# Layer 0's loads written later in the program, four layers' weights loaded one by one, fewer and larger late blocks

## The chip, the cores and the metric

The kernel runs on one core of a Trainium2 chip as a single launch. The metric is the device time in microseconds (us); lower is better.

## The reference

A graph network of four layers over N = 2708 nodes with D = 128 features and one adjacency matrix `adj` of 2708 x 2708 float32, of which under 1% is not zero. Each layer normalises the rows of x, applies relu, and adds its result to x:

```python
h = relu(layernorm(x)); x = x + L0(h, adj)   # (adj.T @ h) / column sums of adj
h = relu(layernorm(x)); x = x + L1(h, adj)   # sum over j of adj[i,j] * gelu(s[i] + d[j] + msg_b), then upd_w, gelu, layernorm
h = relu(layernorm(x)); x = x + L2(h, adj)   # adj @ h, W_msg, relu, then a GRU cell (W_ih, W_hh and biases)
h = relu(layernorm(x)); x = x + L3(h, adj)   # two attention heads over adj > 0 (ff0, attn, ff1, g1, b1, g2, b2)
```

## The kernel before

Rows go in 22 tiles of 128 (the last has 20), in six groups of four tiles (`GROUPS`; the last group has two). The order of work on each engine is the order in which the program is written.

**Layer 0** (up to about 223 us) reads the whole of `adj` once, as 30 sets (c, s), a window of columns c (0 to 4) by a group of rows s (0 to 5), in the order of the list `order`; set 6c + s is its number here. The last 228 columns (window 5, `LAST`) are loaded apart, into `z0` to `z5`, and worked on between the sets of window 4. For each set:

- SP's queue loads `a` (`load_cut`, L318, or L324 for the short group) into a ring of `RING = 5` buffers, so that a load waits for the set five before it.
- DVE finds the eight largest values of each row in every block of 124 columns and their places (`list_cut`, L358 and L360); GpSimd (POOL) masks the blocks near the diagonal first (`mask_near`).
- PE transposes the set (`p_T`, L396) in up to four turns and adds `a` times h to the window's sums (L382). A turn goes into one of three PSUM banks (`turnp`).
- ACT evacuates a turn to `aT` (L401) with the column sums as a by-product, and then issues the write of the turn before it to `adjT` in HBM from its own queue (`write_one`, L366). Layers 2 and 3 read `adjT`.
- When a window is done, DVE inverts its column sums (`inv_deg`, L431), and the window's part of x is formed. After the last window, PE transposes the sums (`p_s`, L449), which waits for a DVE block that ends with `ends` (L637).

Between the sets, ACT also works on rows of x (L254, L264, L136). Every transfer that SP's or ACT's queue issues takes one of eight completion semaphores, in rotation in the order of the program over both queues, and waits until the transfer eight before it, which has the same semaphore, is done. An ACT instruction behind such a write waits with it.

Layer 1's weights are loaded at set 3 (`(c, s) == (0, 3)`, L590 to L593), those of layers 2 and 3 at set 15 (`(2, 3)`, `load` L90 and `load_columns` L97), all from SP's queue.

**Layer 1** (about 255 to 590 us) goes over the 22 row tiles in `period(t)`, each with steps k. For each tile it lists the non-zero entries, gathers the columns' features with matmuls on PE, applies gelu on ACT and adds up again with matmuls. ACT copies the column numbers (`where_T`, L844), which SP passes through HBM (`passed` L846, `spread`). The blocks of 124 columns that layer 0 had no time to list, the late blocks, are loaded from `adj` by `load_late` at k = 4, one period ahead: `AT_ONCE = 5` blocks for a period, each in a transfer of its own (`cols_a`), and listed on DVE by `list_late`. Layers 2 and 3 follow from about 600 us on.

Of the kernel before, what the change touches and what calls it, by code (L numbers as in the profile page):

```python
# [51 lines left out]
def size(t):  # L52
    return min(P, N - t * P)


def width(b):
    return min(JB, N - b * JB)
# [3 lines left out]
def listed_layers(ctx: ExitStack, tc: tile.TileContext, x, adj, w, out, flag):  # L61
# [23 lines left out]
    ident = const.tile([P, P], F32, name="ident")  # L85
    make_identity(nc, ident)

    def load(pool, name, shape=None):
        t = pool.tile(list(shape or w[name].shape), F32, name=name)
        nc.sync.dma_start(t, w[name])  # L90
        return t

    def load_columns(pool, name):

        k = w[name].shape[0] // P
        t = pool.tile([P, k], F32, name=name)
        nc.sync.dma_start(t, w[name].rearrange("(k p) -> p k", p=P), allow_slow_non_contiguous=True)  # L97
        return t

    def load_rows(pool, name):  # L100

        t = pool.tile([P, w[name].shape[0]], F32, name=name)
        nc.sync.dma_start(t, w[name].partition_broadcast(P))
        return t


    minus_half = const.tile([P, NT], F32, name="minus_half")
# [175 lines left out]
            yield  # L283

    RING = 5
    WINDOW = CH + 16 * (len(GROUPS) - 2)
    l0, ending = ExitStack(), ExitStack()
    ordered = ExitStack()
# [253 lines left out]
    for i, (c, s) in enumerate(order):  # L542
        g0, gk = GROUPS[s]
        if i == len(order) - 1:
            for n in range(4):
                list_last(n)
            count_some(0, FIRST)
            count_some(FIRST, 1)
        list_cut(c, s, g0)
        if i == 0:  # L550
            state["f", 0] = factors(*state.pop(("m", -1)))
            list_cut(c, s, g0 + 1)
            state["m", 1] = moments(tiles_of(xs, *GROUPS[1]), "n4")
            list_cut(c, s, g0 + 2)
            state["f", 1] = factors(*state.pop(("m", 1)))
            list_cut(c, s, g0 + 3)
        else:
            for n in range(g0 + 1, g0 + gk):
                if c > 0 and s == (1 if c < LAST - 1 else 0) and n == g0 + 2:
                    invert(c - 1)  # L560
                list_cut(c, s, n)
        if i + 1 < len(order):
            mask_near(*order[i + 1])
        if i > 0 and i - 1 + RING < len(order):
            load_cut(*order[i - 1 + RING])
        if c == LAST - 2:
            load_cut(LAST, s)
        if c > 0 and s == (2 if c < LAST - 1 else 1):
            turn_sums(c - 1)
        if (c, s) == (LAST - 1, LAST):  # L570
            turn_rows(LAST - 2)
            ranked = rank(0, FIRST, bank("p_r"))
            turn_sums(LAST)
        work_cut(c, s, first_steps(s) if c == 0 else next_steps(c, s))
        if c > 1 and s == 0:
            turn_rows(c - 2)
        if c > 1 and s == 1:
            destinations(c - 2)
        if c > 1 and s == 3:
            split_destinations(c - 2)  # L580
        if c == LAST - 1:
            for z in PARTS.get(s, ()):
                mask_near(LAST, z)
                work_cut(LAST, z)
            if s == LAST - 1:
                for _ in lift(LAST):
                    pass

        if (c, s) == (0, 3):
            nc.sync.dma_start(msg_wT, w["msg_wT"])  # L590
            nc.sync.dma_start(upd_wT, w["upd_wT"])
            for v, name in ((upd_b, "upd_b"), (ln_w, "ln_w"), (ln_b, "ln_b"), (msg_b, "msg_b")):
                nc.sync.dma_start(v, w[name].partition_broadcast(P))  # L593
        if (c, s) == (2, 3):
            W_msgT, W_ihT, W_hhT = load(late, "W_msgT"), load(late, "W_ihT"), load(late, "W_hhT")
            b_msg, b_ih, b_hh = load_columns(late, "b_msg"), load_columns(late, "b_ih"), load_columns(late, "b_hh")
            ff0T, ff0, ff1T = load(late, "ff0T"), load(late, "ff0"), load(late, "ff1T")
            attn = load_columns(late, "attn")
            gain1, shift1, gain2, shift2 = (load_columns(late, v) for v in ("g1", "b1", "g2", "b2"))
            nc.gpsimd.tensor_copy(src_self[:, 0, :], msg_wT[:, 0, :])  # L600
            nc.gpsimd.tensor_tensor(src_self[:, 1, :], msg_wT[:, 0, :], msg_wT[:, 1, :], ALU.add)

# [47 lines left out]
    destinations(LAST - 2)  # L650
    l0.close()

    gate_b = late.tile([P, 2], F32, name="gate_b")
    half_b = late.tile([P, 1], F32, name="half_b")

# [20 lines left out]
    with (  # L676
# [25 lines left out]
        def load_late(t):  # L702

            units = late_blocks[(t - 1) * AT_ONCE : t * AT_ONCE] if t > 0 else []
            if not units:
                return
            cols = work.tile([P, AT_ONCE, JB], F32, name="cols_a")
            state["late", t] = []
            for i, (n, b) in enumerate(units):
                m, k = size(n), width(b)  # L710
                nc.sync.dma_start(cols[0:m, i, 0:k], adj[n * P : n * P + m, b * JB : b * JB + k])
                state["late", t].append((n, b, cols[0:m, i, 0:k]))

        def list_late(t, first, last):
            units = state.get(("late", t), [])[first:last]
# [312 lines left out]
        def period(t, between=()):  # L1028

            now, c, b, a = (0 <= t + q < NT for q in range(4))  # L1030
            last = 0 <= t - 1 < NT
            if c and not between:
                put_values(t + 1)
            for k in range(GB):
                for step in between[k : k + 1]:
                    step()
                if now:
                    combine(t, k)
                if k == (0 if t else 1) and c:
                    pass_on(t + 1)  # L1040
                if k == 1 and a:
                    nc.vector.tensor_copy(*rank(t + 3, 1, rpool.tile([P, CH], F32, tag="r", name="p_r")))
                    spread_ends(t + 3)
                if k == 1 and last:
                    gather(t - 1, GB - 2)
                elif k in (3, 5) and now:
                    gather(t, k - 3)
                if now:
                    activate(t, k)
                if k == 1 and last:  # L1050
                    gather(t - 1, GB - 1)
                    close_tile(t - 1)
                elif k in (3, 5) and now:
                    gather(t, k - 2)
                if k == 1:
                    if now and t % 2 == 0 and t + 2 < NT:
                        project(t // 2 + 1)
                if (t, k) in mixes:
                    mix(mixes[t, k])
                if k in (1, 2) and b:  # L1060
                    fetch(t + 2, k - 1)
                if k == 1 and a:
                    lead_of(*values_of(t + 3))
                if k == 1:
                    list_late(t, 0, EARLY)
                    if t == WIDE_AT:
                        list_wide()
                if k == 2:
                    if now and t % 2 == 0 and t + 2 < NT:
                        sources(t // 2 + 1)  # L1070
                    if a:
                        select_rows(t + 3)
                        describe_rest(t + 3)
                    if now and t % 2 == 0 and t + 2 < NT:
                        sources_rest(t // 2 + 1)
                    if now and t + 4 < NT - 2:
                        count_rows(t + 4)
                if k == 1 and t == NT - 2:
                    check_lists()
                if k > 0 and c:  # L1080
                    put_more(t + 1, k)
                if k == 3 and c:
                    columns(t + 1)
                if k == 3 and t == WIDE_AT:
                    place_wide()
                if k == 3 and b:
                    place(t + 2)
                if k == 4 and a:
                    finish_rows(t + 3)
                if k == 4:  # L1090
                    load_late(t + 1)
                    if t + 1 == WIDE_AT:
                        load_wide()
                for g, step in updates.pop((t, k), ()):
                    update(g, step)
                if k == GB - 1:
                    list_late(t, EARLY, AT_ONCE)
                    if now and NT - 2 <= t + 4 < NT:
                        count_rows(t + 4)
# [28 lines left out]
        if True:  # L1128
            period(0)
            for t in range(1, NT + 1):  # L1130
                period(t)
            assert not updates
        puts.close()
    lists.close()

# [874 lines left out]
```

## Time and profile before

| | us |
|---|---|
| median of three runs | 1023.68 (1022.53 to 1025.39) |
| the profiled execution | 1026.56 |
| its span | 1024.8 |
| busy: PE, DVE, ACT, POOL | 925.0, 796.3, 533.6, 460.2 |

The profile is of one execution, on one core. A span of 1024.8 in 40 slices makes one slice 25.6 us. Names like `a` stand for all buffers of that name. The engine SP issues transfers only; its rows are marked SPq, and ACT's issues ACTq. A wait names what ended it, inferred from the semaphores. `adj`'s loads of layer 0 are 1.0 to 1.15 MB for a full set, an `adjT` write 256 KB, a late block 62 KB.

### The profile page before, as it was taken

The page shows a single profiled execution, that of the slowest core. Times are in us where ns is not written, and L with a number is a line of the kernel's source. Part 1 is how long each engine was busy: PE and PEld are TensorE (multiplying, and loading weights), DVE is VectorE, ACT ScalarE, POOL GpSimd, SP SyncE. Part 2 cuts the span into 40 slices and gives each one's busy share as a digit, 9 for nine tenths or more (in the row PEclk, how much of TensorE's full clock was granted, in tenths as well). Part 3 has the DMA queues.
Part 4 walks back from the last instruction along what each step waited for, and adds up shares of the span by engine and source line. Part 5 has one row for each costly group of instructions (what it writes and reads, how often), then busy time and mean ns, then how long its engine had stood idle before and what let it go on. Part 6 is the DMA issues. An engine that isn't in the chain of part 4 may idle for free. (4 is left out here: it accounts for less than half of the span.)

```text
span 1024.8 us, 22209 instructions
## 1 busy us (share of the span) xinstructions
PE 925.0 (90%) x7948; PEld 748.9 (73%) x7948; DVE 796.3 (78%) x2753; ACT 533.6 (52%) x1561; POOL 460.2 (45%) x588
## 2 busy tenths in 40 slices
PE   6699898964899999999899999999889999999983
PEld 3354454733799999999899844444578999989972
DVE  7998784976788898998976566666578977997793
ACT  5655546744667566767666523323322543664342
POOL 6322122322887777897976364433211300340042
PEclk9998989965899999999999999999899999999996
DMA  9899899613244334443332366555311475457000
GB/s 334 266 309 318 263 350 379 224 68 113 75 135 139 123 116 120 131 137 102 109 114 105 108 217 217 176 198 195 85 45 56 144 222 187 139 169 234 7 15 16
DMA packets 88954, 165.42 MB, mean 161 GB/s; under 512 B 20432, under 2 KB 35908, under 8 KB 88834
## 3 DMA queue, kind: packets, MB, share of 16 engines
q1 hardware_dynamic: 68854, 131.77, 40.2%
q10 hardware_dynamic: 19980, 32.14, 8.6%
q8 instruction: 64, 1.05, 0.4%
q14 instruction: 56, 0.46, 0.1%
HBM read 117.26 MB, written 30.87 MB: 145 GB/s over the span
## 5 line engine op out<-in xcount | busy, mean ns | idle before, releaser
L1219 PE MATMUL att<-hv,wt 128*128 128x129 f32 x1672 | 195.5, 278 | 7.4 <-DVE wt L1189 5.9
L825 POOL TENSOR_SCALAR put<-count,line,value 128x128 f32<-128x128 f32 x176 | 195.1, 1120 | 11.7 <-PE agg L938 10.6
L1219 PEld LDWEIGHTS att<-hv,wt 128*128 128x128 f32 x1672 | 191.8, 194 | 10.5 <-DVE wt L1189 8.5
L913 PE MATMUL p_m<-s,sel 128*128 128x128 bf16 x1452 | 162.6, 220 | 6.5 <-ACT g L925 4.0
L917 PE MATMUL p_m<-d,cols 124*128 124x128 bf16 (+1 forms) x1452 | 162.9, 221 | 3.8 <-DVE cols L856 3.8
L1189 DVE SCALAR_TENSOR_TENSOR wt<-row,lift,mask 128x1024 f32<-128x1024 f32 (+1 forms) x132 | 138.8, 1082 | 23.0 <-PE att L1219 22.9
L120 POOL TENSOR_TENSOR n_r<-n_r,minus_half 128x4 f32<-128x4 f32 (+1 forms) x28 | 39.5, 1412 | 243.4 <-DVE n_r L119 238.2
L382 PE MATMUL sums<-a,h 128*128 128x512 f32 x220 | 124.4, 664 | 1.6 <-ACT h L136 1.6
L938 PE MATMUL agg<-put,g 128*128 128x128 f32 (+1 forms) x968 | 122.5, 279 | 0.0
L396 PEld LDWEIGHTS p_T<-ident,a 128*128 128x128 f32 (+1 forms) x440 | 57.3, 149 | 83.2 <-issue 42.7
L938 PEld LDWEIGHTS agg<-put,g 128*128 128x128 f32 x968 | 113.2, 192 | 0.0
L1380 PE MATMUL p_agg<-a,hs 128*128 128x512 f32 (+2 forms) x264 | 107.9, 550 | 3.4 <-DMA a<-adjT 3.4
L913 PEld LDWEIGHTS <-sel 128*128 128x128 bf16 x1452 | 104.1, 98 | 7.9 <-issue 7.2
L917 PEld LDWEIGHTS <-cols 124*128 124x128 bf16 (+1 forms) x1452 | 103.2, 98 | 4.9 <-DVE cols L856 4.9
L925 ACT ACTIVATE g<-p_m 128x512 f32<-128x512 f32 x132 | 72.7, 553 | 59.5 <-PE agg L938 42.8
L834 ACT ACTIVATE put<-mine,value 128x128 f32<-128x128 bf16 x308 | 100.7, 393 | 0.0
L396 PE MATMUL p_T<-ident,a 128*128 128x128 f32 (+1 forms) x440 | 75.2, 292 | 26.7 <-ACT aT L401 20.2
L401 ACT ACTIVATE aT<-p_T 128x512 f32<-128x512 f32 (+2 forms) x132 | 71.0, 539 | 37.4 <-PE p_T L396 27.9
L1380 PEld LDWEIGHTS p_agg<-a,hs 128*128 128x128 f32 (+1 forms) x264 | 47.4, 193 | 50.4 <-issue 45.4
L360 DVE FIND_INDEX8 col<-val,a 128x8 uint16<-128x124 f32 x306 | 82.3, 281 | 0.0
L1342 ACT ACTIVATE hs<-hs 128x1354 f32<-128x1354 f32 (+1 forms) x44 | 58.5, 1329 | 41.6 <-DMA hs<-in_adj 41.2
L358 DVE MAX8 val<-a 128x8 f32<-128x124 f32 x306 | 70.8, 272 | 2.4 <-DMA a<-in_adj 2.4
(291 smaller groups left out, 1568.7 us busy)
## 6 DMA issues: line engine op xcount, KB each, us to landing
hs<-in_adj SPq DMA_DIRECT2D x42, 677.0 KB
adjT<-aT ACTq DMA_DIRECT2D x105, 256.0 KB
a<-adjT SPq DMA_DIRECT2D x20, 1280.0 KB
spread<-passed SPq DMA_DIRECT2D x22, 704.0 KB
later<-sel SPq DMA_DIRECT2D x22, 616.0 KB
a<-in_adj SPq DMA_DIRECT2D x5, 1152.0 KB
a<-in_adj SPq DMA_DIRECT2D x5, 1120.0 KB
a<-in_adj SPq DMA_DIRECT2D x5, 1088.0 KB
```

The source lines that it names most:

```text
L360: nc.vector.max_index(col[0:m, n, b, :], val[0:m, n, b, :], v)
L382: nc.tensor.matmul(accs[c][:, 0:w], h0[0:m, n, :], a[0:m, n - g0, t0 * P - lo : t0 * P - lo + w], start=(n == 0), stop=(n == NT - 1),)
L396: nc.tensor.transpose(p[0:k, i * iw + q * P : i * iw + q * P + m], a[0:m, q, e : e + k], ident[0:m, 0:m])
L825: nc.gpsimd.tensor_scalar(st["put", 0][:, b, :], count, st["line"][:, b : b + 1], st["value"][:, b : b + 1], ALU.is_equal, ALU.mult,)
L834: nc.scalar.activation(st["put", 1][:, b - HP, :], st["mine"][:, b - HP, :], AF.Identity, scale=st["value"][:, b : b + 1])
L913: nc.tensor.matmul(p[:, b - b0, :], st["sel"][:, b, :], s3[:, q, t % 2, :], start=(q == 0), stop=False)
L917: nc.tensor.matmul(p[:, b - b0, :], st["cols"][0:kb, b, :], d3[0:kb, b, q, :], start=False, stop=(q == 2))
L925: nc.scalar.activation(g[:, 0:n, :], state[t].pop(("p", k))[:, 0:n, :], AF.Gelu)
L938: nc.tensor.matmul(agg, g[:, b - 4 * k, :], put, start=(b == 0), stop=False)
L1189: nc.vector.scalar_tensor_tensor(wt[:, 0:n], row[:, k, c : c + n], lift[:, j, k : k + 1], mask[:, j, c : c + n], op0=ALU.max, op1=ALU.mult,)
L1219: nc.tensor.matmul(banks[s // 3][:, s % 3, :], wt[:, q * P : (q + 1) * P], hv[:, j, k, :], start=(v < 2 and s // 3 not in touched), stop=( ...
L1380: nc.tensor.matmul(pa[:, 0:n], h[0:k, j, :], a[0:k, j - j0, 0:n], start=(j == 0), stop=(j == NT - 1))
```

## The change

It has three parts.

- *Layer 0's loads.* In the written program, the load of set j stands at set j − 2 and no longer at set j − 4 (`BEHIND = 2`). The ring still has five buffers. The loads of `z0` to `z5` stay at the sets of window 3, and so come before `a` loads that they came after.
- *Weights.* Of the six transfers at set 3 only `msg_wT` is left, at set 8, and `msg_b`, at set 15. The other 18 (`upd_wT`, `upd_b`, `ln_w`, `ln_b` of layer 1 and all of layers 2 and 3) are put on the list `waiting`; `load_next` issues one of them at k = 0 and one at k = 3 of each period of layer 1 until the list is empty.
- *Late blocks.* Neighbouring blocks of the same tile are loaded in one transfer, and always for 128 rows.

```diff
+    waiting = []
+
+    def load(pool, name):
+        t = pool.tile(list(w[name].shape), F32, name=name)
+        waiting.append((t, w[name], {}))
         return t
...
+    def load_next():
+        if waiting:
+            t, v, how = waiting.pop(0)
+            nc.sync.dma_start(t, v, **how)
...
     RING = 5
+    BEHIND = 2
...
-        if i > 0 and i - 1 + RING < len(order):
-            load_cut(*order[i - 1 + RING])
+        if i > BEHIND and i - 1 - BEHIND + RING < len(order):
+            load_cut(*order[i - 1 - BEHIND + RING])
         if c == LAST - 2:
             load_cut(LAST, s)
...
-        if (c, s) == (0, 3):
+        if (c, s) == (1, 2):
             nc.sync.dma_start(msg_wT, w["msg_wT"])
-            nc.sync.dma_start(upd_wT, w["upd_wT"])
-            for v, name in ((upd_b, "upd_b"), (ln_w, "ln_w"), (ln_b, "ln_b"), (msg_b, "msg_b")):
-                nc.sync.dma_start(v, w[name].partition_broadcast(P))
         if (c, s) == (2, 3):
-            W_msgT, W_ihT, W_hhT = load(late, "W_msgT"), load(late, "W_ihT"), load(late, "W_hhT")
...
+            nc.sync.dma_start(msg_b, w["msg_b"].partition_broadcast(P))
...
+    waiting.append((upd_wT, w["upd_wT"], {}))
+    for v, name in ((upd_b, "upd_b"), (ln_w, "ln_w"), (ln_b, "ln_b")):
+        waiting.append((v, w[name].partition_broadcast(P), {}))
+    W_msgT, W_ihT, W_hhT = load(late, "W_msgT"), load(late, "W_ihT"), load(late, "W_hhT")
...
-                m, k = size(n), width(b)
-                nc.sync.dma_start(cols[0:m, i, 0:k], adj[n * P : n * P + m, b * JB : b * JB + k])
-                state["late", t].append((n, b, cols[0:m, i, 0:k]))
+                state["late", t].append((n, b, cols[0 : size(n), i, 0 : width(b)]))
+            i = 0
+            while i < len(units):
+                n, b = units[i]
+                k = 1
+                while i + k < len(units) and units[i + k] == (n, b + k) and width(b + k) == JB:
+                    k += 1
+                if width(b) < JB:
+                    nc.sync.dma_start(cols[:, i, 0 : width(b)], adj[n * P : (n + 1) * P, b * JB : b * JB + width(b)])
+                else:
+                    nc.sync.dma_start(
+                        cols[:, i : i + k, :],
+                        adj[n * P : (n + 1) * P, b * JB : (b + k) * JB].rearrange("p (b e) -> p b e", e=JB),
+                    )
+                i += k
...
+                if k in (0, 3):
+                    load_next()
                 if k == 4:
                     load_late(t + 1)
```

More of the change, by code (lines that the diff above doesn't have):

```diff
@@ L86, in listed_layers @@
     make_identity(nc, ident)
-    def load(pool, name, shape=None):
-        t = pool.tile(list(shape or w[name].shape), F32, name=name)
-        nc.sync.dma_start(t, w[name])
+    waiting = []
+    def load(pool, name):
+        t = pool.tile(list(w[name].shape), F32, name=name)
+        waiting.append((t, w[name], {}))
         return t
@@ L96, in load_columns @@
         t = pool.tile([P, k], F32, name=name)
-        nc.sync.dma_start(t, w[name].rearrange("(k p) -> p k", p=P), allow_slow_non_contiguous=True)
+        waiting.append((t, w[name].rearrange("(k p) -> p k", p=P), dict(allow_slow_non_contiguous=True)))
         return t
[L100 to L104, printed above, removed]
+    def load_next():
+        if waiting:
+            t, v, how = waiting.pop(0)
+            nc.sync.dma_start(t, v, **how)
     minus_half = const.tile([P, NT], F32, name="minus_half")
@@ L587, in listed_layers @@
                     pass
-        if (c, s) == (0, 3):
+        if (c, s) == (1, 2):
             nc.sync.dma_start(msg_wT, w["msg_wT"])
-            nc.sync.dma_start(upd_wT, w["upd_wT"])
-            for v, name in ((upd_b, "upd_b"), (ln_w, "ln_w"), (ln_b, "ln_b"), (msg_b, "msg_b")):
-                nc.sync.dma_start(v, w[name].partition_broadcast(P))
         if (c, s) == (2, 3):
-            W_msgT, W_ihT, W_hhT = load(late, "W_msgT"), load(late, "W_ihT"), load(late, "W_hhT")
[L596 to L599, printed above, removed]
+            nc.sync.dma_start(msg_b, w["msg_b"].partition_broadcast(P))
             nc.gpsimd.tensor_copy(src_self[:, 0, :], msg_wT[:, 0, :])
@@ L651, in listed_layers @@
     l0.close()
+    waiting.append((upd_wT, w["upd_wT"], {}))
+    for v, name in ((upd_b, "upd_b"), (ln_w, "ln_w"), (ln_b, "ln_b")):
+        waiting.append((v, w[name].partition_broadcast(P), {}))
+    W_msgT, W_ihT, W_hhT = load(late, "W_msgT"), load(late, "W_ihT"), load(late, "W_hhT")
+    b_msg, b_ih, b_hh = load_columns(late, "b_msg"), load_columns(late, "b_ih"), load_columns(late, "b_hh")
+    ff0T, ff0, ff1T = load(late, "ff0T"), load(late, "ff0"), load(late, "ff1T")
+    attn = load_columns(late, "attn")
+    gain1, shift1, gain2, shift2 = (load_columns(late, v) for v in ("g1", "b1", "g2", "b2"))
     gate_b = late.tile([P, 2], F32, name="gate_b")
@@ L1131, in listed_layers @@
                 period(t)
-            assert not updates
+            assert not updates and not waiting
         puts.close()
```

## The prediction

> **What bounds the kernel now.** I read the page's slices first, since the change touches layers 0 and 1 only.
>
> ```profile
> PE   6699898964899999999899999999889999999983
> PEclk9998989965899999999999999999899999999996
> DMA  9899899613244334443332366555311475457000
> ```
>
> A slice is 25.6 us. Layer 0 is the first nine slices, and the only stage where the DMA row stands at 8 or 9 while PE falls under 9 and the clock under full. Layer 1 (slices 10 to 23) has PE at 9 and DMA at 2 to 4. Windows price both; the columns are the stretch, busy PE, PEld, DVE, ACT, POOL, then clock, DMA share and GB/s:
>
> ```profile
> 75.00:80.00 5.00, 5.00 (x25) 2.89 (x24) 5.00 (x34) 2.82 (x12) 0.22 (x1) 1.00 1.04 400
> 126.37:136.50 10.13, 10.10 (x20) 4.62 (x21) 4.55 (x30) 5.46 (x22) 2.80 (x9) 0.50 0.99 323
> 170.87:215.30 44.43, 39.28 (x227) 27.11 (x225) 44.18 (x289) 31.51 (x109) 13.78 (x40) 1.00 0.64 237
> 260.00:560.00 300.00, 290.35 (x4192) 286.04 (x4192) 252.77 (x690) 201.58 (x619) 246.33 (x254) 0.99 0.37 116
> ```
>
> Layer 1 is PE's (290 of 300 us). In layer 0 no engine is full throughout: for 10 us PE works at half its clock, and the last 44.4 us before layer 0's end are DVE's (44.18 busy). What starts that block is in the waits of 0 to 250 us (engine, tile, line, releaser; total, count, longest):
>
> ```profile
> DVE inv_deg L431 <- ACT aT L401: 26.1, 3, 14.5
> PE p_T L396 <- ACT aT L401: 20.6, 17, 2.8
> ACT junk L264 <- DMA a<-in_adj: 7.9, 2, 4.0
> PE p_s L449 <- DVE ends L637: 3.5, 1, 3.5
> ACT junk L264 <- DMA W_hhT<-in_W_hhT: 3.2, 1, 3.2
> ```
>
> PE waits for ACT's evacuations, DVE for ACT's column sums (its longest wait ends at 170.87, after which it runs to 215.29 and releases PE's p_s at 215.43). ACT in turn waits for transfers that its instruction doesn't read: the timeline puts its adjT write just ahead of each stall.
>
> ```profile
> 38.93 0.33 ACTq L366 DMA_DIRECT2D adjT<-aT  x1
> 39.30 0.40 ACT L264 ACTIVATE junk<-xs,flat 128x128 f32<-128x128 f32 x1 [3.92 <-DMA a<-in_adj]
> ...
> 123.59 0.40 ACT L264 ACTIVATE junk<-xs,flat 128x128 f32<-128x128 f32 x1 [3.25 <-DMA W_hhT<-in_W_hhT]
> ...
> 124.71 0.92 PE L396 MATMUL p_T<-ident,a 128*128 128x128 f32 x4 [2.80 <-ACT aT L401]
> 126.40 1.32 PE L396 MATMUL p_T<-ident,a 128*128 128x128 f32 x4 [0.78 <-ACT aT L401]
> ```
>
> In the built program every DMA of both queues takes one of eight semaphores in turn and waits for the one eight before it. So an ACT write stalls ACT until a load or weight on SP's queue lands; ACT's evacuations stand behind it, three PSUM banks later PE stands too, and the clock drops after that. Such ACT stalls sum to some 25 us in layer 0 (3.92 at 35.4, 4.02 at 79.0, 1.62 + 3.25 + 0.63 at 117 to 125, 4.14 at 142.3, 2.46 at 150, 3.20 at 170.8, two under 1).
>
> **What the Trainium skill says.** "TensorE: Matmul & The Clock Gate", "What's actually happening": the clock is halved by default and after an idle window of about 3.4 us, and comes back after a busy one. The trace agrees on the value (0.50) but not on the length: the gap before 126.37 was 2.80 us with 0.78 close behind, and the half clock lasted 10.1 us. "DMA: Bandwidth & Descriptors", "Issuing engines are not separate DMA queues": transfers of all issuers share the same 16 engines. The trace agrees: loads on SP's queue and writes on ACT's together stop at 400 GB/s with the share at 1.04. The same page, "Rules for kernel authors": coalesce many small transfers. Layer 1's late blocks are 62 KB each, but nothing is seen waiting for them.
>
> **The change, part by part.**
>
> *Loads of layer 0 (BEHIND).* In the built programs PE, ACT, DVE and POOL have the same instructions in the same order. The `a` loads keep their order on SP's queue, and each still waits for the set five before it; the SP timeline has most of them 0.03 us behind that buffer's last product already. Loads land 12 to 23 us before PE's first transpose of them. So the two sets by themselves: 0. What moves is `z`: each of the six last-column loads now stands two `a` loads earlier in SP's queue.
>
> *Weights out of layer 0.* Six small transfers at 33.66 to 36.83 become one msg_wT later, and 14 at 114.07 to 126.25 become msg_b alone:
>
> ```profile
> 113.64 0.37 SPq L318 DMA_DIRECT2D a<-in_adj  x1
> 114.07 0.51 SPq L90 DMA_DIRECT2D W_msgT<-in_W_msgT  x1
> ...
> 116.10 0.49 SPq L97 DMA_DIRECT2D b_msg<-in_b_msg  x1
> 120.93 0.38 SPq L97 DMA_DIRECT2D b_ih<-in_b_ih  x1
> ...
> 126.37 5.76 SPq L318 DMA_DIRECT2D a<-in_adj  x3
> ```
>
> - First block (A). With six transfers fewer in the rotation, the write that waited for set 7's load (35.38 to 39.30) becomes one four writes later, by when that load has landed. In its wake set 4 took PE 11.61 us (40.81 to 52.42) against 7.33 for sets 2 and 3, so 4.28, plus the 1.28 ahead of it: 5.6. Early stalls are partly taken up later, so I count 5 (0 to 6).
> - Second block (B). The ACT stalls for adjT, W_hhT and ff0T go, with PE's gaps 2.80 + 0.78 = 3.58, and the half clock 126.37 to 136.50, which costs half its length, 5.1: 8.7; I count 8 (3 to 9). Loads 20 and 21 are no longer held 10.2 and 5.8 us behind free buffers (116.20 to 126.37, 121.91 to 127.69); they were in time anyway, and only relax the queue.
> - `z` earlier (C). The `a` loads 22, 24, 25, now interleaved with the `z` loads, have the ACT write that waits for them only 3 to 5 writes (about 3.5 to 6 us) behind their issue, where loads took 7 to 11 us from issue to landing. ACT stalls like 142.31 to 146.46 and 170.83 to 174.03 come back in other places. The trace of before can't show this: between 0 and 10 us lost, of which I take 3.
> - Bytes. About 1.1 MB leave a stage that runs near its DMA peak: 1.1/400 = 2.8 us, part of A and B, not added.
>
> *Where layer 0's gain can be lost.* The stages from the end of set 23 on are fixed: DVE's block of 44.4 us stays, so what counts is how much earlier ACT ends set 23 (170.84). DVE has room: its three waits at inv_deg sum to 26.1 us, so up to 26 us pass through before DVE's own lists are the limit. After the block the order is as before, PE's clock is low across the change of layers (6 and 5 in slices 9 and 10) in both.
>
> *Weights in layer 1.* 18 transfers, one at k = 0 and one at k = 3 of the first nine periods, on SP's queue. In front of them SP mostly waits for ACT, as its waits in 255 to 600 us show, and DMA is at 0.37.
>
> ```profile
> SPq L846 <- ACT where_T L844: 100.3, 20, 15.1
> ```
>
> At 0.4 to 0.9 us an issue (rows above) 18 cost SP about 9 us over nine periods of some 15 us. Cover: SP's wait for where_T. The first used (upd_wT) is needed periods after it was issued, layer 2's at about 600. 0 (0 to 3 lost, if a weight holds up SP's index transfers behind it).
>
> *Late blocks.* 80 transfers become 21: 59 issues fewer on SP at some 0.5 us, so 30 us off a queue that waits 100 us, and 2480-byte rows for 496-byte ones. Nothing waits for them: 0 (0 to 2 gained).
>
> **Sum.** 5 + 8 − 3 = 10 gained. The profiled execution is 1026.56 (span 1024.8 and 1.76 around it): 1016.6. That execution is 2.88 above the median, 1023.68, so **1013.7** against the runs.
>
> **Rivals.**
>
> 1. *Nothing to speak of.* The rotation stays, so ACT's stalls find other loads; layer 0 as a whole moves its bytes at about 310 GB/s against 400. For: the stall 79.0 to 83.0 (load 13, issued 72.26) stands in the built order as before, and nothing touches it. Then only the bytes count: 1023.68 − 3 = about 1021. On the edge of what can be told. That the change doesn't do what it says is half true: the loads' two sets do nothing in the built order.
> 2. *Slower.* With z loads interleaved between loads 22 to 26, five ACT stalls of about 4 us each replace two. PE tolerates 2.4, so five gaps of 1.6 = 8, and each second one brings a half-clock window of about 10 us, which costs 5: 13 more, 21 lost in sets 16 to 23 against 13 won: 1023.68 + 8 = about 1031. This decides where loads take over about 6.3 us from issue while their write is four behind; against it, without the weights these loads find less on the engines, and DVE's 14.46 us of room takes nothing, because set 23 itself would be late.
> 3. *More.* Relieved from set 7 on, the loads run earlier and the stall at 79.0 to 83.0 with the half clock at 85.3 to 95.5 goes too: PE's gap there 1.54 + 10.2/2 = 6.6, and C costs nothing: 5 + 8 + 6.6 = 20: about 1004.
>
> **How the numbers follow.** My forecast has 0.50, rival 3 has 0.20, rival 1 has 0.17, rival 2 has 0.13. 0.3% of 1023.68 is 3.1 us, about what a measurement of this kernel can tell from no change. Forecast and rival 3 lie below 1020.6, and a third of rival 1: faster 0.74. The rest of rival 1, and a part of 2: same 0.14. Slower 0.12. The range goes from rival 3 (1003) to just past no change (1025), leaving out most of rival 2 and what is beyond 20 gained.
>
> **What would show it.** Right: no ACT wait on a weight; full clock at 47.7 to 51.1 and 126 to 136; DVE's waits at inv_deg down from 26.1 to about 16 with its last one ending near 160; then again a block of 44 us, PE's p_s at about 205, layers 1 to 3 as long as before. Wrong: new ACT waits on DMA z or a between 125 and 165 (rival 2), or a layer 1 that grows, with SP or DVE waiting for cols_a or a weight.

## The result, and the profile after

The changed kernel takes 1017.24 us (1016.58 to 1017.67) against 1023.74 us: a ratio of 0.9935, with a 95% interval of 0.9918 to 0.9952. That is 6.5 us faster; the forecast was 1013.7, 10 us faster, in a range of 1003 to 1025. A second measurement beside its parts (e7 below) gave 0.9941 (0.9920 to 0.9961).

The profiled execution took 1016.94 us with a span of 1015.1, 9.6 us under the one shown of before. Single executions of the kernel before, 35 of them beside e1 to e4, ran from 1019.36 to 1030.73, so a difference of two traces is not yet the difference of two kernels; the second trace of before (e11) will matter for that.

The page's slices after (25.4 us each):

```profile
PE   6799898945899999999899999999889999999983
PEclk9998999955999999999999999999899999999996
DMA  9899998413444443434223266655301574457000
```

DMA stands at 8 or 9 up to the seventh slice, as before, and is down to 4 in the eighth, where it was at 6: layer 0's traffic ends earlier. The clock of the sixth slice (127 to 152 us) is up from 8 to 9. Some of the waits of 0 to 250 us follow (engine, tile, line, releaser; total, count, longest). Line numbers here are those of the changed kernel: in layer 0 most are one or two larger, and L637 is now L632.

```profile
DVE inv_deg L433 <- ACT aT L403: 22.1, 3, 12.8
PE p_T L398 <- ACT aT L403: 19.6, 14, 3.1
ACT hT L152 <- DMA a<-in_adj: 4.8, 1, 4.8
ACT hs L137 <- DMA z<-in_adj: 4.7, 1, 4.7
PE p_s L451 <- DVE ends L632: 4.5, 1, 4.5
ACT part_x L462 <- DMA a<-in_adj: 4.1, 1, 4.1
ACT junk L265 <- DMA a<-in_adj: 3.8, 1, 3.8
```

No weight is among the releasers any more. But ACT's waits on transfers haven't shrunk: summed over 20 to 185 us they are 27.0 us before and 28.8 after. They stand behind other transfers now.

The stretches that the prediction named, in the windows (busy PE, PEld, DVE, ACT, POOL, clock, DMA share, GB/s):

```profile
47.70:51.10 3.40, 3.40 (x12) 1.57 (x13) 3.40 (x25) 1.38 (x11) 3.00 (x11) 1.00 0.96 200
126.37:136.50 10.13, 9.77 (x41) 5.44 (x40) 10.13 (x70) 5.34 (x17) 3.91 (x14) 0.83 1.08 389
162.80:207.03 44.23, 37.72 (x219) 26.11 (x217) 43.98 (x289) 30.78 (x109) 13.58 (x40) 0.98 0.59 223
260.00:560.00 300.00, 293.52 (x4247) 289.56 (x4244) 250.63 (x688) 202.20 (x619) 243.44 (x252) 1.00 0.38 122
```

The half clock is gone from the first stretch and mostly from the second, where it covers 3.4 of the 10.1 us and PE now does 41 instructions in place of 20. DVE's last block starts 8.1 us earlier (162.80 for 170.87) and has the same length (44.23 for 44.42). Its end releases PE's p_s at 207.17, 8.3 us earlier than 215.43.

PE's instructions are the same in both kernels, so the end of the n-th matmul of a tile can be set against its counterpart. PE's lead over the first trace of before, in us:

| at (us of before) | 30 | 55 | 75 | 100 | 132 | 150 | 190 | 250 | 560 | 720 | 750 |
|---|---|---|---|---|---|---|---|---|---|---|---|
| lead | 0.0 | 5.7 | 4.5 | 5.4 | 12.5 | 8.9 | 9.3 | 8.2 | 8.2 | 7.7 | 9.6 |

The lead comes in two steps, at the places of the two weight blocks (the second reaches 13.6 at 135), and each step is partly given back within 20 us. Layer 1 adds and takes nothing in this pair of traces: 8.2 at both its ends.

### The profile page after: what moved, and what is told of

Read it like the earlier page. It is cut to its first block, busy times and chain, and to the rows that moved or that the text cites. A ratio compares the mean times of both kernels' runs of the same rounds, so it can differ in the third digit from the quotient of the medians.

```text
span 1015.1 us, 22140 instructions
## 1 busy us (share of the span) xinstructions
PE 915.4 (90%) x7948; PEld 743.6 (73%) x7948; DVE 795.6 (78%) x2753; ACT 531.3 (52%) x1561; POOL 458.8 (45%) x588
## 5 line engine op out<-in xcount | busy, mean ns | idle before, releaser
L840 POOL TENSOR_SCALAR put<-count,line,value 128x128 f32<-128x128 f32 x176 | 198.8, 1141 | 11.6 <-PE agg L953 10.5
L384 PE MATMUL sums<-a,h 128*128 128x512 f32 x220 | 118.9, 637 | 1.6 <-ACT h L137 1.6
L398 PE MATMUL p_T<-ident,a 128*128 128x128 f32 (+1 forms) x440 | 72.4, 286 | 25.6 <-ACT aT L403 19.2
```

The source lines that it names most:

```text
L384: nc.tensor.matmul(accs[c][:, 0:w], h0[0:m, n, :], a[0:m, n - g0, t0 * P - lo : t0 * P - lo + w], start=(n == 0), stop=(n == NT - 1),)
L398: nc.tensor.transpose(p[0:k, i * iw + q * P : i * iw + q * P + m], a[0:m, q, e : e + k], ident[0:m, 0:m])
L840: nc.gpsimd.tensor_scalar(st["put", 0][:, b, :], count, st["line"][:, b : b + 1], st["value"][:, b : b + 1], ALU.is_equal, ALU.mult,)
```

## The experiments

Theory: the gain is that ACT no longer stands behind weight transfers in layer 0; the z loads' earlier place costs some of it; late blocks and the weights in layer 1 are free. Rivals: the z loads' order, or layer 1, carries a good part. A third rival has no run: that the weights' bytes, 1.1 MB less in a stage with a DMA share of 0.92, count by themselves, whoever stalls (the prediction put them at 2.8 us, as a part of A and B). The measured ratios, each to runs of the kernel before on the same chip:

| | kernel | us | ratio (95%) |
|---|---|---|---|
| e1 | before + weights moved | 1015.37 | 0.9919 (0.9894 to 0.9944) |
| e2 | before + loads two sets later | 1026.57 | 1.0027 (1.0004 to 1.0050) |
| e3 | before + late blocks merged | 1022.55 | 0.9984 (0.9965 to 1.0002) |
| e4 | changed, loads as before | 1015.34 | 0.9910 (0.9887 to 0.9934) |
| e5 | before + first weight block moved | 1022.18 | 0.9979 (0.9965 to 0.9993) |
| e6 | before + second block moved | 1019.30 | 0.9952 (0.9936 to 0.9967) |
| e7 | changed, again | 1018.32 | 0.9941 (0.9920 to 0.9961) |
| e8 | e4 + adjT writes on SP's queue | 1015.00 | 0.9915 (0.9884 to 0.9947) |
| e9 | e4 + z two loads later | 1014.29 | 0.9889 (0.9860 to 0.9918) |
| e10 | e8 + seven aT buffers | 1009.11 | 0.9835 (0.9810 to 0.9860) |
| e12 | e10 + z two loads later | 1005.92 | 0.9815 (0.9791 to 0.9838) |

### The parts one by one (e1 to e4)

e1 has the change's hunks for the weights alone; e3 has the one in `load_late` alone. e2 and e4 differ from before and from the changed kernel in one number each:

```diff
 # e2, in the kernel before
-        if i > 0 and i - 1 + RING < len(order):
-            load_cut(*order[i - 1 + RING])
+        if i > 2 and i - 3 + RING < len(order):
+            load_cut(*order[i - 3 + RING])
 # e4, in the changed kernel
-    BEHIND = 2
+    BEHIND = 0
```

> The kernel before with the weights moved alone (both blocks; loads of a and z written as before, late blocks in single transfers). My theory, that the whole gain comes from ACT no longer standing behind weight transfers in layer 0: about 6 to 8 us under the kernel before, so 1016 to 1018, with PE's lead over before 5.7 us at set 5 and 9 to 10 us at set 23, as in the changed kernel. Rival, that z and the late blocks carry half of it: about 1020.

> The kernel before with the loads of layer 0 written two sets later alone; in the built program only the six z loads move, each two a loads earlier. My theory: no gain, since the weights still stand ahead of load 20 and the ACT stalls at 35 and 117 to 125 stay: 1022 to 1027. Rival, that freeing the order of the z loads is where the gain comes from: 1018 to 1020.

> The kernel before with the late blocks of a tile in one transfer alone (21 for 80). My theory: nothing waits for them and SP's queue has 100 us to spare in layer 1, so within 1 us of the kernel before. Rival, that SP's queue or DVE's wait for cols_a matters in layer 1: 2 to 3 us faster, with layer 1 shorter by that.

> The changed kernel with the loads of layer 0 written as before (BEHIND = 0): weights moved and late blocks merged. If the z loads' earlier place costs the 3 us that the prediction set for it: about 1014. If it costs nothing: 1017, as the changed kernel. If it is needed for the gain: 1020.

The weights alone bring 9.0 us between medians, more than the whole change. The loads written two sets later cost 2.2 between medians when made alone, and taking them out of the change (e4) gains as much as the weights alone. Late blocks: the interval holds no change, so they may be worth up to 3.6 us or nothing; that e4, which has them, is no faster than e1 makes nothing the likelier. So of the three parts one carries the gain and one takes some of it back.

That the two sets move the z loads alone, as the prediction and e2's expectation have it, is not so. Whatever SP's queue issues between the `a` loads now stands two of them earlier. In e2 the block of six starts at 21 us in place of 34, and the block of 14 at 92 in place of 114; in the changed kernel `msg_wT` goes out at 53.49, in e4 at 63.61. So e2, and the step from e4 to the changed kernel, price z together with these.

What the gain consists of can be read from PE. It does the same work in the same order in all these kernels, so its time from one matmul to another is its idle time plus its busy time, and its busy time for the same work differs with the clock. The windows go from the product that ends at 29.8 us to the last of the eight transposes that start at 166.37 in the first trace of before (set 23). They are of before, e11 (before again), e1, the changed kernel and e7 (changed again), in this order:

```profile
29.79:167.96 138.17, 122.57 (x494) 67.70 (x492) 110.50 (x733) 81.22 (x306) 37.73 (x109) 0.90 0.92 309
29.80:162.17 132.37, 117.03 (x493) 65.42 (x492) 110.25 (x734) 79.58 (x301) 36.94 (x107) 0.94 0.94 318
29.84:157.78 127.94, 115.06 (x493) 64.53 (x492) 110.08 (x733) 80.11 (x305) 37.11 (x108) 0.95 0.92 324
29.80:158.32 128.52, 114.24 (x493) 64.25 (x492) 109.96 (x733) 78.98 (x301) 36.93 (x107) 0.96 0.94 323
29.70:155.45 125.75, 111.53 (x493) 63.05 (x492) 109.84 (x733) 78.91 (x301) 37.08 (x107) 0.99 0.96 333
```

Length less busy time is the idle time. With layer 0 as before it is 15.6, 15.3 and, in e3, 15.7 us; with the weights out 12.9 (e1) and 12.4 (e4); in the changed kernel 14.3 and 14.2. So the weights take some 3 us out of PE's waits, and the loads' part puts 1.3 to 1.9 back. The rest is the clock: take off the share of the length that it withheld (0.10 of 138.17 in the first line), and 109 to 110 us of busy time remain in each. Of the 9.6 us between the first trace of before and that of the changed kernel, 8.3 are busy time. This part differs between executions of one program by 5.5 us (before) and 2.7 us (changed). But the mean granted clock, listed for every run, goes the same way: 0.947 and 0.948 over 35 and 47 runs of before, 0.951 in e1 and in e4, 0.954 and 0.955 in the changed kernel and e7.

### The two weight blocks (e5, e6), and the change again (e7)

e5 leaves the block of 14 at set 15 and moves the rest; e6 leaves the block of six at set 3:

```diff
 # e5, at set 15
+            W_msgT, W_ihT, W_hhT = load(late, "W_msgT"), load(late, "W_ihT"), load(late, "W_hhT")
...
+            while waiting:
+                load_next()
 # e6, at set 3 (and not at sets 8 and 15)
+            nc.sync.dma_start(msg_wT, w["msg_wT"])
+            nc.sync.dma_start(upd_wT, w["upd_wT"])
...
```

> The kernel before with the first weight block moved alone: upd_wT, upd_b, ln_w, ln_b to layer 1, msg_wT to set 8, msg_b to set 15; the second block of 14 stays at set 15, and layer 1 loads four weights. My theory, that the early ACT stall at 35 us (5.7 us of PE) is passed on to the end in part: 3 to 5 us faster than before. Rival, that it is taken up again by the stalls behind the second block, so that only the second block counts: within 1 us.

> The kernel before with the second weight block (14 transfers at 114 to 126 us) moved to layer 1 alone; the first block stays at set 3. My theory: 4 to 6 us faster, about half of the 9 us that both blocks bring. Rival, that the second alone carries all of it: 8 to 9 us.

> The changed kernel once more, beside its parts. If the z loads' earlier place costs what its own run showed (2.2 us) on top of weights and late blocks: about 6.5 to 7 us faster than before. If weights alone and all three parts are one and the same within the noise: 9 us faster.

The first block is worth 2.1 us (0.7 to 3.6), the second 4.9 (3.4 to 6.6), both 8.3 (5.7 to 10.9). In e5's trace PE leads by 5.7 us after set 4, as in the changed kernel, but then meets the second block:

```profile
118.88 0.40 ACT L265 ACTIVATE junk<-xs,flat 128x128 f32<-128x128 f32 x1 [5.18 <-DMA W_ihT<-in_W_ihT]
```

```profile
120.00 1.32 PE L398 MATMUL p_T<-ident,a 128*128 128x128 f32 x4 [4.72 <-ACT aT L403]
```

The first line is of ACT's timeline, the second of PE's. ACT came earlier to a write that is bound to a weight, and waited longer for it; PE's gap grew from 2.80 to 4.72, and its lead fell from 6.4 to 4.5 (4.1 at 150). Here a lead won ahead of a fixed stall was in part waited away at it.

e7 repeats the changed kernel's own 0.9935.

### The place of the z loads (e9), and what still holds ACT (e8, e10, e12)

```diff
 # e9 and e12: z two sets later
-        if c == LAST - 2:
-            load_cut(LAST, s)
+        if 0 <= i - 2 - len(GROUPS) * (LAST - 2) < len(GROUPS):
+            load_cut(LAST, i - 2 - len(GROUPS) * (LAST - 2))
 # e8, e10, e12: the adjT writes from SP's queue
-            nc.scalar.dma_start(*written.pop())
+            nc.sync.dma_start(*written.pop())
 # e10, e12
-    turned = l0.enter_context(tc.tile_pool(name="l0t", bufs=6))
+    turned = l0.enter_context(tc.tile_pool(name="l0t", bufs=7))
```

> The changed kernel with BEHIND = 0 and the adjT writes issued from SP's queue and not from ACT's: ACT never waits for the completion semaphore of a load, SP does. My theory, that ACT's stalls behind transfers are what remains between layer 0 and full speed: ACT's waits on DMA a and z (about 20 us in the changed kernel) go, PE's half-clock windows before 200 us go, and the kernel is 5 to 15 us faster than the changed one (1002 to 1012). Rival, that the stall only changes its place, since SP now holds the writes behind a load and ACT runs out of its six aT buffers: same or slower, with ACT waiting on DMA adjT.

> The changed kernel with BEHIND = 0 and the six z loads two a loads later than before (four later than in the changed kernel). If the earlier a z load stands the more it takes from the a loads and ACT's writes, as the runs so far suggest (2 to 3 us from two places): about 2 us faster than without the move, so 11 us under the kernel before, about 1013. Rival, that it is only chance which ACT write falls behind which load: 1014 to 1020, with another list of ACT waits.

> The kernel with the adjT writes on SP's queue and seven aT buffers instead of six. There ACT waited 25 us on DMA adjT in 13 waits, for want of a free aT. One more buffer covers one turn (1.3 us) of each. If these waits carry the time: ACT's waits fall to 10 to 15 us and the kernel is 3 to 5 us faster than with six (1010 to 1012). Rival, that the 16 DMA engines set the rate of layer 0 in 50 to 170 us and the wait only shows where it is felt: under 1 us faster, with waits that come back elsewhere (PE or DVE on DMA a, or ACT still over 20 us).

> The kernel with seven aT buffers and the adjT writes on SP's queue, and besides the six z loads two a loads later than before. If the z loads' place costs by itself, whatever queue the writes are on: 1 to 2 us faster than with z as before (ratio to the kernel before 0.982). If its cost came only through ACT's writes that fall behind a load, which are gone here: the same as with z as before, 0.9835, within 0.002.

The place of z: two loads earlier 0.9935 and 0.9941, as before 0.9910, two loads later 0.9889. The three stand in order, 2 to 3 us a step; the neighbours' intervals overlap, the ends' (0.9918 to 0.9952 and 0.9860 to 0.9918) touch. With e2, which is slower than before by more than its interval, it is shown that the loads' part costs time, 2.2 us between e2's medians (0.4 to 5.1 by its interval). That z's place costs by itself is not: only e9 and e12 move z alone, and each is some 2 us faster than its counterpart (e4, e10), within the intervals.

The traces have two places where the changed kernel's PE waits longer than e4's. The first is behind `msg_wT`, not z. SP's timeline, then PE's:

```profile
53.49 0.34 SPq L592 DMA_DIRECT2D msg_wT<-in_msg_wT  x1
```

```profile
60.62 0.66 PE L398 MATMUL p_T<-ident,a 128*128 128x128 f32 x4 [1.04 <-ACT aT L403]
```

ACT waits here for load 10 in both kernels. With `msg_wT` two loads earlier the write that waits falls ahead of an evacuation; in e4 it falls ahead of a copy of the window's sums, and PE has no gap. In e7 the gap is 1.17. The second place is behind z0, which the changed kernel issues at 111.28:

```profile
111.28 0.64 SPq L320 DMA_DIRECT2D z<-in_adj  x1
116.06 0.37 SPq L320 DMA_DIRECT2D a<-in_adj  x1
```

ACT's timeline has what waited for it:

```profile
124.01 0.33 ACTq L368 DMA_DIRECT2D adjT<-aT  x1
124.39 0.49 ACT L137 ACTIVATE hs<-xs,flat 128x128 f32<-128x128 f32 x1 [4.70 <-DMA z<-in_adj]
```

PE's gap behind this was 3.05 us in the changed kernel and 3.26 in e7; without the move z0 goes out at 123.16, and e4's gap at that place (ending at 128.57, behind load `a`) is 1.99. The two places make 2.1 us (2.4 in e7), about what PE's idle time shows. A further gap, 1.75 at 172.71 and 1.64 in e7, has no counterpart in e4, but lies inside DVE's last block, at whose end PE still waits 4.5 us, so it costs nothing. Nor do the traces show the cost at the end of layer 0: p_s starts at 207.17 and 204.32 in the changed kernel, at 205.52 in e4 and 206.23 in e1, because the clock was better in the first two (0.96 and 0.99 in the windows above, 0.95 in e1 and e4). Whether z's part is the transfers' order or the bytes brought forward into 110 to 165 us, where the DMA share is near 1 already (0.97 in 100 to 165), these runs don't separate.

e8 takes ACT's writes away from loads altogether, and tells what the stall turns into:

```profile
ACT aT L403 <- DMA adjT<-aT: 25.1, 13, 3.7
```

This is the only wait of ACT on DMA in 20 to 185 us, as long as the several together were (25.0 in e4): SP now holds the writes behind loads, and ACT runs out of its six aT buffers. The rival was right; the time is e4's. One more buffer (e10) lowers that sum only to 23.8 us in 11 waits, yet DVE's waits for inv_deg fall from 19.7 to 16.3, and the kernel gains 5.9 us more between medians, 8 in ratio (0.9915 to 0.9835). So neither expectation fits: the time moved further than in the first, the wait as in the second. Seven buffers with the writes on ACT's queue were not run, so the gain is the buffer's, and what SP's queue has to do with it is open. With z later on top (e12) it is 0.9815, which the intervals don't part from e10, so the question that e12 was to answer stays open too. In the profiled execution of e12 ACT's waits on DMA are 20.6, and DVE's for inv_deg 15.6:

```profile
DVE inv_deg L433 <- ACT aT L403: 15.6, 3, 10.7
```

e12 beats both kernels, at 1005.92 us.

### The kernel before once more (e11)

> The kernel before once more, for a second trace of it. If single executions differ in layer 0's stalls: PE stands 1 to 4 us ahead of the first trace from some set on, and a half-clock window is longer or shorter. If they differ in the changes of layers: the lead comes at about 590 or 740 us.

The second trace of before (1022.82 us) stands level with the first up to 80 us and 4.7 us ahead of it at 100. The program is the same, and so is PE's gap, 1.54 us before 84.15 in the first and 1.37 before 83.92 in the second. PE's timeline in the first trace, then in the second:

```profile
84.15 2.17 PE L396 MATMUL p_T<-ident,a 128*128 128x128 f32 x8 [1.54 <-ACT aT L401]
86.25 4.08 PE L382 MATMUL sums<-a,h 128*128 128x512 f32 x4
```

```profile
83.92 1.87 PE L396 MATMUL p_T<-ident,a 128*128 128x128 f32 x8 [1.37 <-ACT aT L401]
85.72 2.18 PE L382 MATMUL sums<-a,h 128*128 128x512 f32 x4
```

In the first the four products take twice as long: its clock was 0.50 from 85.3 to 95.5. In the second the same stretch is at full clock:

```profile
85.30:95.50 10.20, 10.14 (x45) 5.53 (x45) 5.88 (x41) 6.13 (x24) 6.60 (x23) 1.00 1.04 358
```

The changes of layers nearly cancel. At about 590, the end of layer 1, the second trace loses 2.1 (4.6 to 2.5), and at 740, the start of layer 3, it gains 1.9 (2.1 to 4.0), just as the changed kernel's trace does there (7.7 to 9.6). The first trace of before was slow in that place, which the change has no part in.

The half clock at 126 us, which the prediction priced, is in the second trace as well: clock 0.50 in 121.6 to 131.8.

## Why the prediction was right, step by step

- *Where the time comes from: right in the main.* ACT stands behind SP's transfers through the shared semaphores; without the weights in layer 0, ACT's stalls at the two weight blocks go, with PE's gaps behind them. The lead passes through set 23 and DVE's fixed block to the end, and layer 1 returns none of it (8.2 at both ends; 11.0 and 10.6 in e7's trace). But ACT's waits as a whole are as long as before, and the greater part of PE's gain comes by the last link of the chain, the clock: 8.3 of 9.6 us in the first pair of traces. How much is due to the 1.1 MB less, and not to the stalls, is open. inv_deg's last wait ended at 162.80 (forecast about 160), p_s started at 207.17 (about 205), DVE's waits at inv_deg came down to 22.1, where 16 was forecast.
- *First block (A), 5 counted, 2.1 measured* (0.7 to 3.6). The gain on the spot was as worked out, 5.7 us at set 5. What I undersized is what is taken up again: in e5 1.9 us at the next stall (lead 6.4 to 4.5). The 1.3 us that the changed kernel loses at 60 us (5.7 to 4.5) belong to the loads' part: e1, e4 and e5 keep 5.6 to 5.7 up to 75. The 0 to 6 given as bounds holds it.
- *Second block (B), 8 counted, 4.9 measured* (3.4 to 6.6). Here too the gain on the spot was about as worked out: the lead rose from 5.4 at 110 to 13.6 at 135, by 8.2 where 8.7 was worked out. The half-clock stretch in it was no accident of one execution: it is in all four traces of kernels with the block at that place (before, e11, e3, e5), 10 to 14 us long. What I undersized is again what is taken up: in the changed kernel 9.4 of lead were left at 140, and in e1 and e4 half clock comes later, for 10 and 14 us from 155.7 and 154.2. The other stretch, at 85.3 to 95.5, is the one that comes and goes: e11 lacks it, and of the changed kernel's traces the first has its counterpart (0.50 in 82.0 to 88.8) and e7 has none. The prediction counted that one in rival 3 alone.
- *z earlier (C), 3 lost, 2 to 3 measured for the loads' part*: 0.9935 and 0.9941 against e4's 0.9910, and 2.2 in e2. Right in sign and size, but in part by luck. The two sets by themselves were put at 0 with z as all that moves; `msg_wT` moves too, and its place is 1.0 of the 2.1 us that PE waits longer. Of the new ACT waits on z and a, of 4.7, 4.8 and 4.1 us, only the first is z's cost: the third stands in e1 and e4 as well (4.5 and 4.3), and the second lies in DVE's block.
- *Weights in layer 1, late blocks: 0.* e3's interval holds no change, and e1 equals e4. Right within what was measured.
- *The sum.* 5 + 8 − 3 = 10 against 6.5. The two terms of the weights are 13 together in it; measured together (e1) they are 8.3, or 9.0 between medians. That is the miss. On the spot 5.6 and 8.7 were worked out, 14.3 in all, of which the prediction let 1.3 be taken up again by the stalls behind; it was some 5 to 6. That the two profiled executions lie 9.6 apart, near the forecast, is luck: two of the kernel before lie 3.7 apart.
- *Rivals.* Rival 2 described what z does (new stalls between 110 and 172 us) but gave it 21 us for what cost about 2.5: of its five stalls of about 4 us three came, one of them without the z move too, and with them one short half-clock stretch (0.83 over 120 to 130). Rival 3's relief of the stall at 79.0 did not come: ACT waited 3.8 us there after as before. Rival 1's remark that the stalls find other loads is true of ACT's waits (27.0 to 28.8 us), and nearly so of PE's idle time in layer 0 (15.6 to 14.3), but PE lost less to the clock behind them.

## What to carry to other kernels

Look for waits that an engine takes on for a transfer that it doesn't use: in this program the instruction behind a DMA issue stalls until the DMA's semaphore predecessor lands, and moving any transfer, were it one small weight, shifts who waits for whom. Moving small early loads out of such a stage is worth what their stalls cost at the end of the stage, not where they stand: here about 0.6 of the local gain was left (8.3 to 9.0 of 14.3 us), with further stalls behind. Where PE's clock halves after a short gap, look at a second trace before counting it: of two such stretches here one came in all four traces that have its stall, the other in one of two traces of the same program. And split an engine's gain into idle time and busy time: the waits' table alone hid that most of this one was the clock.

## What was not expected of the hardware

- After a PE gap of 1.4 to 1.5 us at the same place of the same program, the clock was halved for 10.2 us in one execution and not at all in another (0.50 and 1.00 in 85.3 to 95.5). In the changed kernel a gap of 2.16 us at 80.31 was followed by the half clock, and one of 1.67 at 79.87 in e7 was not. "TensorE: Matmul & The Clock Gate" of the Trainium skill ("What's actually happening") speaks of an idle window of about 3.4 us, and of windows that run free of the kernel. That about the same gap is caught in one execution and not in another fits the second; that a gap of under half a window is caught at all does not fit the first.
- One more 2 KB-a-partition aT buffer, with the writes on SP's queue, was worth 0.8% of the whole kernel, though ACT's waits for such a buffer fell by 1.3 us of 25.1 in the profiled executions. Medians of 1015.00 and 1009.11 were each taken over six runs, and the profiled execution of e10 was its slowest (1016.7), so its trace doesn't show the gain, though PE's idle time up to set 23 falls from 11.9 (e8) to 10.6 us; what e10's faster executions do differently stays open.
